# Queries of layers 1 to 3 as one pair in step: four of seven products by seven of their own

## The chip, the cores and the metric

The kernel runs on one core of one Trainium2 chip. The metric is the device time of one execution in microseconds. The kernel before takes 2476.75 us, the median of three runs (2476.53 to 2476.88).

## The reference

The program is a small graph network with four attention layers. `x` has 1024 rows of 512; `cond` has 16 sequences of 256 rows of 512; there are 8 heads of 64. Cut to what matters:

```python
def _attn(xf, cond, Wq, Wk, Wv, Wo):
    xb = xf.reshape(BS, n // BS, d)
    q = (xb @ Wq).reshape(BS, -1, H, DH)
    k = (cond @ Wk).reshape(BS, -1, H, DH)
    v = (cond @ Wv).reshape(BS, -1, H, DH)
    att = jnp.einsum('bnhd,bmhd->bhnm', q, k) * DH ** (-0.5)
    w = jax.nn.softmax(att, axis=-1)
    o = jnp.einsum('bhnm,bmhd->bnhd', w, v).reshape(BS, -1, H * DH)
    return (o @ Wo).reshape(n, d)

h = _gcn(batchnorm(relu(layernorm(x))), src, dst, gcn_in_w, gcn_in_b, n)
for i in range(L):                                   # L = 4
    h = h + _attn(_ln(h, ln2_w[i], ln2_b[i]), cond, Wq[i], Wk[i], Wv[i], Wo[i])
    u = _ln(h, ln3_w[i], ln3_b[i]) @ geglu_w[i] + geglu_b[i]
    val, gate = jnp.split(u, 2, axis=-1)
    h = h + (val * gelu(gate)) @ ffo_w[i] + ffo_b[i]
out = x + _gcn(h, src, dst, gcn_out_w, gcn_out_b, n) + x_in
```

All data is 32-bit floating point. The change concerns `q = _ln(h) @ Wq`, the factor `DH ** -0.5`, and what stands around them at the start of layers 1 to 3.

## The kernel before, in words

Seven products for eight. Each large product of the layers is cut into two by two blocks and made from seven products of blocks instead of eight, after Strassen and Winograd: sums of the left blocks, sums of the right blocks, seven products, and sums of the results on their way out of PSUM. A product over a block is a `multiply` (L297 to L305): two matmuls, one for each half of the contraction, for each 128 output rows. A 32-bit matmul appears in the profile as two records.

In step. Of the seven products, four (numbers 0, 5, 6, 4, in the list `INNER`) can be cut once more in the same way. `InStep` does this: `seven_of` runs seven inner products for two outer products at a time, each 128 x 256 wide, and `run` copies their sums back into PSUM banks, on top of which the three remaining outer products (1, 3, 2) add. The class `Pair` uses it for the gated unit (runs r of 1 to 3) and `KeyPair` for the keys of later attention steps. `inner_left` and `inner_right` (L963, L970) make the sums that this needs; they run on GpSimd (POOL). `Pair` keeps its intermediate results in the tile `wos`, which in the attention part holds the sums of `Wo` (`wo_sums`, L836).

One layer. There are 8 attention steps g, each for two sequences of `cond` and 128 rows of h. The start of layers 1 to 3 is written as: the keys and values of step 0 (`kv`), with the norms of the last blocks of h beside them; the transposes `turn_first` of the last four blocks, on whose way out of PSUM the norm's weight and bias columns (`cols`) are applied; the sums of the transposed inputs `lnT` into `lnS` (`sum_first`), for blocks 0 and 1 on POOL and for 2 and 3 on VectorE (DVE); POOL makes also the sums of `Wq` (`weight_sums`). Then the `queries`: two `QueryPair`s, one for each 128 rows of a block of q, with seven products of two matmuls of 512 columns each, the scale being applied in the evictions. Then `wo_sums` on POOL. Then the loop over the steps: `scores` (four banks of scores, the softmax's largest value and normalisation on DVE, exponentials on ScalarE, ACT), at g = 0 the keys and values of step 1, and then `mix`, which transposes the probabilities and multiplies by the values.

The order. Instructions run in order on each engine. The order on each engine is made by a scheduler when the program is built, from the program's order, a cost model and tile dependencies; `tc.issue_after`, `waiting_for` and `tc.keep_in_program_order` bind it. Tiles come from pools: `slots` (36 pieces of 128 x 1024), `work` (10 of 128 x 512, `t512`), `accs` (6), and 8 banks of PSUM. SyncE (SP) issues nearly all DMAs, in order.

For layer 0 the keys of step 1 already stand before the queries; it keeps its form of the queries.

Of the kernel before, what the change touches and what calls it, by code (L numbers as in the profile page):

```python
# [17 lines left out]
P = 128  # L18
# [5 lines left out]
def gnn_kernel(  # L24
# [76 lines left out]
    def slots_of(n, name):  # L101
        return [slot(f"{name}_{i}") for i in range(n)]
# [641 lines left out]
    def values(l, g, wv, begun=None, **also):  # L744
        v, s1 = begun or (slots_of(2, f"v_{l}_{g}"), None)
        v11, v21, v12, v22 = blocks_out(v)
        seven(f"v_{l}_{g}", of_v(wv, conds[l, g]), v11, v12, v21, v22, s1, **also)
        return v
# [218 lines left out]
        sums_of_a(t, *blk, s1, s2, s4)  # L967
        return order7(blk, s1, s2, s4)

    def inner_right(t, b11, b12, b21, b22, room):  # L970

        t1, t2, t3, t4 = (room[:, k, j * M:(j + 1) * M] for k in range(2) for j in range(2))
        for to, of, less in ((t1, b12, b11), (t3, b22, b12), (t2, b22, t1), (t4, b21, t2)):
            t.tensor_tensor(to, of, less, OP.subtract)  # L974
        return [b11, b21, b22, t4, t1, t2, t3]
# [4 lines left out]
        return {i: inner_left(nc.gpsimd, left[i], *rooms[3 * n:3 * n + 3])  # L980
                for n, i in enumerate(INNER[0] + INNER[1])}

    def inner_right_of(i, right, room):
        return inner_right(nc.gpsimd, *(right[i][:, k, n * M:(n + 1) * M]
                                        for k in range(2) for n in range(2)), room)

    class InStep:

# [66 lines left out]
    class Pair(InStep):  # L1055
# [38 lines left out]
        def upper(self, q, d, w7):  # L1094
            self.of_upper[q] = self.gated(q, d, w7, "g1")
# [54 lines left out]
    def cond_rights(l, g):  # L1150

        rooms = slots_of(4, f"kr_{l}_{g}")
        of = conds[l, g], conds[l, g + 1]
        return {i: inner_right(nc.gpsimd, *(x[i][:, k, :] for k in range(2) for x in of), room)
                for i, room in zip(INNER[0] + INNER[1], rooms)}

    def pairs_of(l, r, left, right, inner):
# [73 lines left out]
        product(2, d, False)  # L1231
        add(h12, d)

    class QueryPair:


        def __init__(self, l, c, left, right, qT):
            self.n, self.c, self.left, self.right = f"{l}_{c}", c, left, right
            (self.q11, self.q21), (self.q12, self.q22) = ([qt[d][:, c, :] for d in range(2)]
                                                          for qt in qT)  # L1240

        def product(self, i, to, start):
            multiply(to, self.left[i], self.right[i],
# [2 lines left out]
        def first(self):  # L1246
            self.a = bank(f"qa_{self.n}")
            self.product(0, self.a, True)
            self.s1 = acc_tile(f"qs1_{self.n}")
            nc.scalar.mul(self.s1, self.a, DH ** -0.5)  # L1250

        def second(self):
            self.product(1, self.a, False)
            nc.scalar.mul(self.q11, self.a, DH ** -0.5)

        def rest(self):
            def add(to, of, term):
                nc.vector.scalar_tensor_tensor(to, of, DH ** -0.5, term, OP.mult, OP.add)

            b, c, d = (bank(f"{x}_{self.n}") for x in ("qb", "qc", "qd"))  # L1260
            u2, u3 = (acc_tile(f"{x}_{self.n}") for x in ("qu2", "qu3"))
            self.product(5, b, True)
            add(u2, b, self.s1)
            self.product(6, c, True)
            add(u3, c, u2)
            self.product(4, d, True)
            add(self.q22, d, u3)
            self.product(3, c, False)
            add(self.q21, c, u2)
            self.product(2, d, False)  # L1270
            add(self.q12, d, u2)

    def queries(l, wq):
        qT = [slots_of(2, f"qT_{l}_{i}") for i in range(2)]
        right = [lnT[0][0], lnT[0][1], lnT[1][1], lnS[2], lnS[0], lnS[1], lnT[1][0]]
        pairs = [QueryPair(l, c, wq, right, qT) for c in range(2)]
        for q in pairs:
            q.first()
        for q in pairs:
            q.second()  # L1280
        for q in pairs:
            q.rest()
        return qT

    def sum_first(t, nb):

        c0 = nb % 4 * P
        of = [lnT[i][k][:, :, c0:c0 + P] for k in range(2) for i in range(2)]
        return sums_of_b(t, *of, *(x[:, :, c0:c0 + P] for x in lnS))
# [23 lines left out]
    def turn_first(l, blocks):  # L1313

        for nb in blocks:
# [3 lines left out]
            else:  # L1319
                pt = transposed(xn, f"hT_{nb}")  # L1320
                for k in range(2):
                    nc.scalar.copy(lnT[nb // 4][k][:, :, c0:c0 + P],
                                   four(pt)[:, 2 * k:2 * k + 2, :])

    lnT = [slots_of(2, f"ln2T_0_{i}") for i in range(2)]
    aggregate(parts_in, "in", into_h_and_norm)
    graph.close()
# [34 lines left out]
    for l in range(L):  # L1362

        wk, wv, wq, wo, ffb, spare = projections
        if l:
            lnS = slots_of(3, f"ln2S_{l}")
            kv_next = kv(l, 0, wk, wv, lambda _: ready_first(l, left_to_turn[2:]))
            with waiting_for(scaled.last, mybir.EngineType.Pool):
                sum_first(nc.gpsimd, 0)
                sum_first(nc.gpsimd, 1)  # L1370
                wq = weight_sums(wq, f"wqs_{l}")
                summed = weight_sums.last
            turn_first(l, left_to_turn)
            next_cond(l, 1)
            sum_first(nc.vector, 2)
            sum_first(nc.vector, 3)
        else:
            lnS = slots_of(3, f"ln2S_{l}")
            roots = []

            def root_beside(ins):
                with tc.issue_after(ins.ins):
                    roots.append(deviations(mv_first[1], "ln2_0_4"))

            kT, last_key = keys(0, 0, wk, begun["k0"], root_beside)
            with tc.issue_after(last_key.ins):
                scale_first(1, *roots)
            turn_first(0, [0, 1, 2, 3])
            with waiting_for(scale_first.last, mybir.EngineType.Pool):
                wq = weight_sums(wq, "wqs_0")  # L1390
            kv_next = kT, values(0, 0, wv, begun["v0"])
            turn_first(0, [4, 5, 6, 7])
            sum_first(nc.gpsimd, 0)
            summed = sum_first(nc.gpsimd, 1)
            kT_1, last_key = keys(0, 1, wk, begun["k1"])
            with tc.issue_after(last_key.ins):
                sum_first(nc.vector, 2)
                sum_first(nc.vector, 3)
        qT = queries(l, wq)
        with tc.issue_after(summed.ins):  # L1400
            wo7 = wo_sums(wo)

        ln3T, ln3S, right = [], [], []

# [67 lines left out]
        for g in range(NG - 1):  # L1472
# [26 lines left out]
            if l and g % 2:  # L1499
                with waiting_for(scores.last, mybir.EngineType.Pool):  # L1500
                    key_rights = cond_rights(l, g + 1)

                def kept_moments(ins):
                    if g > 1:
                        with tc.issue_after(ins.ins):
                            moments_into(mv_kept[:, 2 * (g - 3):2 * (g - 1)], [h[g - 3], h[g - 2]],
                                         f"ln3_{l}_{g - 3}")

                vs[g + 1] = values(l, g + 1, wv, beside=kept_moments)
            elif l and g:  # L1510
                turned = range(g) if g == NG - 2 else []
                if turned:
                    with waiting_for(scores.last, mybir.EngineType.Pool):
                        left = geglu_weights(l, 0, *raw)
                vs[g + 1] = values(l, g + 1, wv, late=lambda: [ln3_turn(nb) for nb in turned])
                next_cond(l, g + 2)
                next_cond(l, g + 3)
            else:
                if g or l:
                    kT, vs[g + 1] = kv(l, g + 1, wk, wv, between,  # L1520
                                       late=lambda: [ln3_turn(nb) for nb in ready])
                else:
                    kT, vs[1] = kT_1, values(0, 1, wv)
                kTs[g + 1] = whole(kT)
                save_conds()
                next_cond(l, g + 2)
                if l:
                    next_cond(l, g + 3)
                    spare.append(rows.tile([P, D], F32, tag="last", name=f"spare_{l}"))
                    wk_lefts = inner_lefts(wk, [x[:, i * P:(i + 1) * P] for x in spare  # L1530
                                                for i in range(4)])
# [48 lines left out]
        for r in range(R):  # L1580
# [7 lines left out]
            if r:  # L1588
                fT, fS, quads = pairs_of(l, r, left, right, (lefts, rights))
            else:  # L1590
                wff = []

                rooms = slots_of(4, f"gr_{l}")

                def beside(c):
                    with waiting_for(quads[c].last, mybir.EngineType.Pool):
                        if c < 2:
                            for i in INNER[c]:
                                rights[i] = inner_right_of(i, right, rooms.pop(0))
                    if c == 2:  # L1600
                        wff.extend(out_weights(nc.vector, l, 0, raw_out))

# [83 lines left out]
```

## Time and profile before

| | us |
|---|---|
| runs, median of three | 2476.75 |
| the profiled execution | 2477.14 |
| its span, from the first to the last instruction | 2475.4 |
| TensorE (PE) busy | 2454.0 |
| DVE busy | 1543.6 |
| POOL busy | 807.9 |
| ACT busy | 692.4 |

PE is the matmul stream, PEld the weight loads that run beside it. In a timeline a row has the start in us from the span's start, the length, the engine, the line in the kernel, the operation, output <- inputs, shapes, and the count of instructions merged into the row; in brackets stands how long the engine was idle before it and what ended that. The lengths of TensorE's records overlap from one to the next, since matmuls are pipelined: the distance from start to start is what one costs. In a table of stretches, each row has the stretch, its length, and the busy time and count of PE, PEld, DVE, ACT and POOL, then the granted clock of TensorE, the share of DMA and GB/s. In a table of groups stand the count, the busy time and the mean length of one in ns. In a row of waits stand the total in us, the number of times and the longest.

### The profile page before, as it was taken

The page shows a single profiled execution, that of the slowest core. Times are in us where ns is not written, and L with a number is a line of the kernel's source. Part 1 is how long each engine was busy: PE and PEld are TensorE (multiplying, and loading weights), DVE is VectorE, ACT ScalarE, POOL GpSimd, SP SyncE. Part 2 cuts the span into 40 slices and gives each one's busy share as a digit, 9 for nine tenths or more (in the row PEclk, how much of TensorE's full clock was granted, in tenths as well). Part 3 has the DMA queues.
Part 4 walks back from the last instruction along what each step waited for, and adds up shares of the span by engine and source line. Part 5 has one row for each costly group of instructions (what it writes and reads, how often), then busy time and mean ns, then how long its engine had stood idle before and what let it go on. Part 6 is the DMA issues. An engine that isn't in the chain of part 4 may idle for free. (4 is left out here: it accounts for less than half of the span.)

```text
span 2475.4 us, 33973 instructions
## 1 busy us (share of the span) xinstructions
PE 2454.0 (99%) x12968; PEld 1865.6 (75%) x12968; DVE 1543.6 (62%) x3199; ACT 692.4 (28%) x1564; POOL 807.9 (33%) x883
## 2 busy tenths in 40 slices
PE   7999999999999999999999999999999999999999
PEld 5678887677778887577787888477787888577775
DVE  9655656566675557666675556666684556666661
ACT  7322322122212334122212333222222333322221
POOL 0322223532432223533541224344522222544410
PEclk9999999999999999999999999999999999999999
DMA  5313223110212221111212222011121031111110
GB/s 178 133 39 107 98 76 105 52 35 17 98 35 77 86 68 61 35 50 35 88 45 73 73 77 69 23 46 51 35 98 69 27 111 52 52 51 52 52 68 35
DMA packets 70395, 162.97 MB, mean 66 GB/s; under 512 B 5880, under 2 KB 6208, under 8 KB 70224
## 3 DMA queue, kind: packets, MB, share of 16 engines
q1 hardware_dynamic: 68128, 155.28, 18.8%
q0 software_dynamic: 1376, 4.30, 0.5%
q8 instruction: 107, 1.75, 0.3%
q10 hardware_dynamic: 720, 1.11, 0.1%
q14 instruction: 64, 0.52, 0.1%
HBM read 137.60 MB, written 23.07 MB: 65 GB/s over the span
## 5 line engine op out<-in xcount | busy, mean ns | idle before, releaser
L220 POOL TENSOR_TENSOR ges<-wgate,wgate 128x1024 f32<-128x1024 f32 x16 | 37.7, 2354 | 438.5 <-DVE fs L1176 401.4
L780 ACT ACTIVATE pr<-sc,nmax 128x256 f32<-128x256 f32 x256 | 118.0, 473 | 157.8 <-DVE nmax L775 157.5
L302 PE MATMUL pa_v<-wv,ct 128*128 128x256 f32 x512 | 123.5, 383 | 0.0
L302 PE MATMUL fa<-wff,fT 128*128 128x256 f32 x512 | 121.6, 379 | 0.0
L302 PE MATMUL pc_v<-wv,ct 128*128 128x256 f32 x512 | 121.0, 379 | 0.0
L302 PE MATMUL pd_v<-wvs,ct 128*128 128x256 f32 x512 | 120.9, 379 | 0.0
L302 PEld LDWEIGHTS fa<-wff,fT 128*128 128x128 f32 x512 | 97.3, 190 | 21.8 <-issue 9.6
L302 PEld LDWEIGHTS pa_v<-wv,ct 128*128 128x128 f32 x512 | 95.6, 190 | 19.5 <-issue 6.2
L1010 ACT COPY gs<-ga 128x512 f32<-128x512 f32 x48 | 27.9, 582 | 287.7 <-PE ga L1003 287.7
L974 POOL TENSOR_TENSOR kr<-ct,ct 128x256 f32<-128x256 f32 x36 | 27.7, 769 | 245.5 <-DVE pr L785 245.5
L302 PEld LDWEIGHTS pd_v<-wvs,ct 128*128 128x128 f32 x512 | 97.3, 190 | 13.2
L302 PEld LDWEIGHTS pc_v<-wv,ct 128*128 128x128 f32 x512 | 96.7, 190 | 12.8
L302 PE MATMUL ga<-ln3T,wval 128*128 128x512 f32 x224 | 104.4, 594 | 0.0
L775 DVE TENSOR_REDUCE nmax<-sc 128x2 f32<-128x512 f32 x128 | 82.9, 679 | 31.5 <-PE sc L768 31.5
L1084 ACT ACTIVATE g<-g,gcols 128x512 f32<-128x512 f32 x96 | 69.3, 722 | 94.8 <-DVE g L1081 94.8
L785 DVE TENSOR_SCALAR pr<-pr,inv 128x256 f32<-128x256 f32 x256 | 81.2, 359 | 2.9
L1429 POOL TENSOR_TENSOR hall<-hall,ffb 128x512 f32<-128x512 f32 x32 | 40.0, 1273 | 117.5 <-DVE fs L1176 71.2
L1211 DVE TENSOR_TENSOR hall<-fd,hall 128x512 f32<-128x512 f32 x64 | 44.1, 689 | 54.2 <-PE fd L302 54.2
L302 PE MATMUL gc<-ln3S,wgate 128*128 128x512 f32 x160 | 75.2, 592 | 0.0
L1211 DVE TENSOR_TENSOR hall<-fc,hall 128x512 f32<-128x512 f32 x64 | 44.0, 687 | 41.6 <-PE fc L302 41.6
L302 PEld LDWEIGHTS ga<-ln3T,wval 128*128 128x128 f32 x224 | 41.3, 190 | 35.9 <-issue 34.4
L803 PEld LDWEIGHTS po<-pT,v 128*64 128x64 f32 x2048 | 62.3, 138 | 7.7 <-issue 7.7
(476 smaller groups left out, 6182.6 us busy)
## 6 DMA issues: line engine op xcount, KB each, us to landing
ct<-cond_dram SPq DMA_DIRECT2D x72, 512.0 KB, 5.4
wval<-in_L_gnn_geglu_w_dram SPq DMA_DIRECT2D x32, 512.0 KB, 3.8
wgate<-in_L_gnn_geglu_w_dram SPq DMA_DIRECT2D x32, 512.0 KB, 4.6
wff<-in_L_gnn_ffo_w_dram SPq DMA_DIRECT2D x32, 512.0 KB, 3.8
cond_dram<-ct SPq DMA_DIRECT2D x24, 512.0 KB, 3.1
cond<-in_L_gnn_cond_dram SPq DMA_DIRECT2D x32, 256.0 KB, 4.5
ct<-cond_dram SPq DMA_DIRECT2D x24, 256.0 KB, 5.7
wk<-in_L_gnn_Wk_dram SPq DMA_DIRECT2D x8, 512.0 KB, 4.2
```

The costliest lines, as they stand in the source:

```text
L220: t.tensor_tensor(s1, a21, a22, OP.add)
L302: each(nc.tensor.matmul(at, left[:, k, l0:l1], right[:, k, r0:r1], start=start and n == 0 and k == 0, stop=n == len(cols_of) - 1 and k == ...
L775: nc.vector.tensor_reduce(nmax, ps3, AX.X, OP.max, negate=True)
L780: nc.scalar.activation(pr3[:, a, :], ps3[:, a, :], AF.Exp, bias=nmax[:, a:a + 1], accum_out=tot[:, a:a + 1])
L785: scores.last = nc.vector.tensor_scalar(pr3[:, a, :], pr3[:, a, :], inv[:, a:a + 1], None, OP.mult)
L803: mix.last = nc.tensor.matmul(po[j * DH:(j + 1) * DH, n0:n0 + NPG], v[b][:, m, c * P + j * DH:c * P + (j + 1) * DH], pTs[j][:, at:at + NPG ...
L974: t.tensor_tensor(to, of, less, OP.subtract)
L1010: nc.scalar.copy(s1, a)
L1084: nc.scalar.activation(g, g, AF.Gelu, bias=gate)
L1211: nc.vector.tensor_tensor(to, halves_of(of), to, OP.add)
L1429: nc.gpsimd.tensor_tensor(h[nb], h[nb], ffb, OP.add)
```

## The change

The old `QueryPair` is renamed `QueryQuad` and stays in layer 0. A new `QueryPair(InStep)` makes the queries of layers 1 to 3: products 0, 5, 6 and 4 as two runs of seven inner products, then products 1, 3 and 2. Its inner sums are made on POOL: those of the weights (`wq_lefts`, 16 differences of 128 x 128, behind `weight_sums`) and those of the inputs (`rights`, 16 differences of 128 x 256, in eight pieces of `work`). It keeps its intermediate results in `wos`, so `wo_sums` moves behind it, in layers 1 to 3 to the first step behind the scores. The keys of step 1 are made in front of the queries in all layers, and step 0 of the loop makes the values alone. The scale `DH ** -0.5` leaves the evictions and is multiplied once into the first 32 columns of `cols`, the weights and biases of the norm ahead of the attention.

```diff
+    def quarters(room):
+        return [room[:, k, j * M:(j + 1) * M] for k in range(2) for j in range(2)]
-    def inner_right(t, b11, b12, b21, b22, room):
-        t1, t2, t3, t4 = (room[:, k, j * M:(j + 1) * M] for k in range(2) for j in range(2))
+    def inner_right(t, b11, b12, b21, b22, rooms):
+        t1, t2, t3, t4 = rooms
         for to, of, less in ((t1, b12, b11), (t3, b22, b12), (t2, b22, t1), (t4, b21, t2)):
...
+    def blocks_of_q(qT, c):
+        return [[qT[n][d][:, c, :] for n in range(2)] for d in range(2)]
-    class QueryPair:
+    class QueryQuad:
...
-            nc.scalar.mul(self.s1, self.a, DH ** -0.5)
+            nc.scalar.copy(self.s1, self.a)
...
-                nc.vector.scalar_tensor_tensor(to, of, DH ** -0.5, term, OP.mult, OP.add)
+                nc.vector.tensor_tensor(to, of, term, OP.add)
...
+    class QueryPair(InStep):
+        x = "q"
+        def __init__(self, l, left, right, inner, qT):
+            self.n, self.left, self.right, self.inner = f"{l}", left, right, inner
+            self.w = [wos[:, 2 * q:2 * q + 2, :] for q in range(2)]
+            self.to = [blocks_of_q(qT, c) for c in range(2)]
+        def step(self, i, k):
+            lefts, rights = self.inner
+            return lefts[i][k], rights[i][k]
+        def product(self, i, q, to):
+            multiply(to, self.left[i], self.right[i], [(q * P, (q + 1) * P, 0, 512)], False,
+                     tc.keep_in_program_order)
+        def first(self, q, a):
+            nc.scalar.copy(self.to[q][0][0], a)
+        def upper(self, q, d, w7):
+            nc.vector.tensor_tensor(self.to[q][1][1], d, w7, OP.add)
+        def lower(self, q, c, w7, a):
+            nc.vector.tensor_tensor(self.to[q][1][0], c, w7, OP.add)
+        def final(self, q, d):
+            nc.scalar.copy(self.to[q][0][1], d)
-    def queries(l, wq):
+    def queries(l, wq, lefts=None):
         qT = [slots_of(2, f"qT_{l}_{i}") for i in range(2)]
         right = [lnT[0][0], lnT[0][1], lnT[1][1], lnS[2], lnS[0], lnS[1], lnT[1][0]]
+        if lefts:
+            rooms = [t512(f"qr_{l}_{i}") for i in range(8)]
+            rights = {i: inner_right_of(i, right, [x[:, j * M:(j + 1) * M]
+                                                   for x in rooms[2 * n:2 * n + 2]
+                                                   for j in range(2)])
+                      for n, i in enumerate(INNER[0] + INNER[1])}
+            QueryPair(l, wq, right, (lefts, rights), qT).run()
+        else:
...
+    nc.vector.tensor_scalar(cols[:, :2 * L * KC], cols[:, :2 * L * KC], DH ** -0.5, None, OP.mult)
     lnT = [slots_of(2, f"ln2T_0_{i}") for i in range(2)]
...
                 wq = weight_sums(wq, f"wqs_{l}")
-                summed = weight_sums.last
+                rooms = [weight_sums.spare, *(t512(f"ql_{l}_{i}") for i in range(2))]
+                wq_lefts = inner_lefts(wq, [x[:, i * P:(i + 1) * P] for x in rooms
+                                            for i in range(4)])
             turn_first(l, left_to_turn)
             next_cond(l, 1)
             sum_first(nc.vector, 2)
             sum_first(nc.vector, 3)
+            kT_1, _ = keys(l, 1, wk)
+            qT = queries(l, wq, wq_lefts)
         else:
...
-        qT = queries(l, wq)
-        with tc.issue_after(summed.ins):
-            wo7 = wo_sums(wo)
+            qT = queries(l, wq)
+            with tc.issue_after(summed.ins):
+                wo7 = wo_sums(wo)
...
-                if g or l:
+                if g:
                     kT, vs[g + 1] = kv(l, g + 1, wk, wv, between,
                                        late=lambda: [ln3_turn(nb) for nb in ready])
                 else:
-                    kT, vs[1] = kT_1, values(0, 1, wv)
+                    kT, vs[1] = kT_1, values(l, 1, wv)
+                    if l:
+                        with waiting_for(scores.last, mybir.EngineType.Pool):
+                            wo7 = wo_sums(wo)
```

More of the change, by code (lines that the diff above doesn't have):

```diff
@@ L981, in inner_lefts, with inner_right_of @@
                 for n, i in enumerate(INNER[0] + INNER[1])}
-    def inner_right_of(i, right, room):
-        return inner_right(nc.gpsimd, *(right[i][:, k, n * M:(n + 1) * M]
-                                        for k in range(2) for n in range(2)), room)
+    def inner_right_of(i, right, rooms):
+        return inner_right(nc.gpsimd, *quarters(right[i]), rooms)
     class InStep:
@@ L1153, in cond_rights @@
         of = conds[l, g], conds[l, g + 1]
-        return {i: inner_right(nc.gpsimd, *(x[i][:, k, :] for k in range(2) for x in of), room)
+        return {i: inner_right(nc.gpsimd, *(x[i][:, k, :] for k in range(2) for x in of), quarters(room))
                 for i, room in zip(INNER[0] + INNER[1], rooms)}
@@ L1232, in ffn_out @@
         add(h12, d)
-    class QueryPair:
+    def blocks_of_q(qT, c):
+        return [[qT[n][d][:, c, :] for n in range(2)] for d in range(2)]
+    class QueryQuad:
         def __init__(self, l, c, left, right, qT):
             self.n, self.c, self.left, self.right = f"{l}_{c}", c, left, right
-            (self.q11, self.q21), (self.q12, self.q22) = ([qt[d][:, c, :] for d in range(2)]
-                                                          for qt in qT)
+            self.to = blocks_of_q(qT, c)
         def product(self, i, to, start):
@@ L1249, in first @@
             self.s1 = acc_tile(f"qs1_{self.n}")
-            nc.scalar.mul(self.s1, self.a, DH ** -0.5)
+            nc.scalar.copy(self.s1, self.a)
         def second(self):
             self.product(1, self.a, False)
-            nc.scalar.mul(self.q11, self.a, DH ** -0.5)
+            nc.scalar.copy(self.to[0][0], self.a)
         def rest(self):
             def add(to, of, term):
-                nc.vector.scalar_tensor_tensor(to, of, DH ** -0.5, term, OP.mult, OP.add)
+                nc.vector.tensor_tensor(to, of, term, OP.add)
             b, c, d = (bank(f"{x}_{self.n}") for x in ("qb", "qc", "qd"))
@@ L1266, in rest @@
             self.product(4, d, True)
-            add(self.q22, d, u3)
+            add(self.to[1][1], d, u3)
             self.product(3, c, False)
-            add(self.q21, c, u2)
+            add(self.to[1][0], c, u2)
             self.product(2, d, False)
-            add(self.q12, d, u2)
-    def queries(l, wq):
+            add(self.to[0][1], d, u2)
+    class QueryPair(InStep):
[18 more added lines that the diff above has]
+            nc.scalar.copy(self.to[q][0][1], d)
@@ L1274, in queries @@
+    def queries(l, wq, lefts=None):
         qT = [slots_of(2, f"qT_{l}_{i}") for i in range(2)]
         right = [lnT[0][0], lnT[0][1], lnT[1][1], lnS[2], lnS[0], lnS[1], lnT[1][0]]
[L1276 to L1282, printed above, removed]
+        if lefts:
[6 more added lines that the diff above has]
+        else:
+            quads = [QueryQuad(l, c, wq, right, qT) for c in range(2)]
+            for q in quads:
+                q.first()
+            for q in quads:
+                q.second()
+            for q in quads:
+                q.rest()
@@ L1598, in beside @@
                             for i in INNER[c]:
-                                rights[i] = inner_right_of(i, right, rooms.pop(0))
+                                rights[i] = inner_right_of(i, right, quarters(rooms.pop(0)))
                     if c == 2:
```

## The prediction

> **What bounds the kernel now.** I read the page's totals first, then who TensorE waited for, then the order of time around the queries of layer 1.
>
> ```profile
> span 2475.4 us, 33973 instructions
> PE 2454.0 (99%) x12968; PEld 1865.6 (75%) x12968; DVE 1543.6 (62%) x3199; ACT 692.4 (28%) x1564; POOL 807.9 (33%) x883
> PE hw_in L463 <- ACT h0T L455: 2.2, 1, 2.2
> ```
>
> TensorE is busy 99% of the span. Its waits of 2 us and more all lie ahead of layer 0; the row shown (us in total, times, longest), where it waits once for the normalised input, returns below. In the layers it waits for nobody. So the change is worth what it takes off TensorE, less every gap that it opens there. The other engines matter through such gaps alone. In order of time, layer 1:
>
> ```profile
> 722.54 1.91 PE L184 MATMUL tr_ln<-ident,xn_ln 128*128 128x128 f32 x16
> 724.29 7.03 PE L302 MATMUL qa<-ln2T,wq 128*128 128x512 f32 x16
> 731.16 1.88 PE L302 MATMUL qb<-ln2S,wqs 128*128 128x512 f32 x4
> 748.42 1.96 PE L768 MATMUL sc<-kT,qT 64*64 64x256 f32 x32
> 750.31 1.99 PE L302 MATMUL pa_k<-ct,wk 128*128 128x256 f32 x8
> 774.59 1.91 PE L184 MATMUL tr_pr<-ident,pr 128*128 128x128 f32 x16
> ...
> 1295.25 7.03 PE L302 MATMUL qa<-ln2T,wq 128*128 128x512 f32 x16
> 1319.38 0.88 PE L768 MATMUL sc<-kT,qT 64*64 64x256 f32 x12
> ...
> 1866.21 7.03 PE L302 MATMUL qa<-ln2T,wq 128*128 128x512 f32 x16
> 1890.34 1.96 PE L768 MATMUL sc<-kT,qT 64*64 64x256 f32 x32
> ```
>
> From the first query product to the scores pass 24.13 us in each of layers 1 to 3 (748.42 - 724.29, and so on), so what is found for layer 1 counts three times. A matmul of 32-bit data stands as two records. The queries have 28 matmuls of 512 columns, 56 records, and records of this width follow each other every 0.429 us ((731.16 - 724.29) / 16): 24.04 us, and 0.09 at the seam. There is no slack in it. Durations in the rows overlap; I count from start to start.
>
> **Removed and put in: TensorE.** Four of the seven products (16 matmuls of 512 columns) become, for each of two outer pairs, seven inner products of two matmuls of 256: 28 matmuls, 56 records. The other three products stay: 12 matmuls, 24 records of 512. The gated unit's pair already runs exactly this sequence, so its stretches are the price:
>
> ```profile
> 724.29:748.33 24.04, 24.04 (x58) 10.46 (x56) 11.69 (x24) 5.70 (x11) 2.45 (x2) 1.00 0.00 1
> 627.68:639.76 12.08, 12.08 (x57) 10.64 (x56) 8.08 (x12) 4.46 (x8) 11.85 (x15) 1.00 0.28 99
> 639.76:650.06 10.30, 10.30 (x25) 4.56 (x24) 6.19 (x11) 3.99 (x6) 0.30 (x1) 1.00 0.00 1
> ```
>
> The first row is the queries as they are, the second the two sets of seven, the third the last six products. 24.04 - 12.08 - 10.30 = 1.66, with the steps unrounded 1.65 us a layer, 4.95 in all. That is the whole gain that this change can have on TensorE. It is also, to a hundredth, the 0.2% (4.95 us) below which I call a difference none, since about that much is what a measurement of this kernel can tell from no change. So the forecast hangs on whether anything of it is lost.
>
> **Moved: the keys of the second step.** Their 28 matmuls, two ACT copies and five DVE adds go from behind the scores to in front of the queries; no DMA goes with them, and SP's order of issues is unchanged. Their cond tiles must be there 26 us earlier, at 724.29:
>
> ```profile
> 691.64 4.25 SPq L280 DMA_DIRECT2D ct<-cond_dram  x4
> DMA to landing us min/median/max: 2.1/5.1/18.6
> ```
>
> The last of the four is issued by 695.9 and even the slowest landing of the run, 18.6, makes 714.5. Free. Behind the scores now stand the values alone: the seam after the scores (0.10 us: 750.31 to the next product took 1.83 in place of 1.73) stays, with pa_v in it. The cover of the first softmax falls from 24 to 12 us. Step 1 of the same layer runs that way already:
>
> ```profile
> 778.44 1.96 PE L768 MATMUL sc<-kT,qT 64*64 64x256 f32 x32
> 784.70 0.62 DVE L785 TENSOR_SCALAR pr<-pr,inv 128x256 f32<-128x256 f32 x2
> 792.52 0.71 PE L184 MATMUL tr_pr<-ident,pr 128*128 128x128 f32 x5
> ```
>
> The probabilities are done 6.9 us behind the first score (784.70 + 0.62), the transposes begin 14.1 behind it, without a gap. ACT's last query copies and the table load before its exponentials come later than today; I put that at some 0.5 us, and 7 us are free. Cost 0.
>
> **Scale in the norm's columns.** The evictions lose a factor; DVE waits for TensorE ahead of each, so a shorter one gives nothing. One DVE instruction is added, in the set-up, between the last two row statistics:
>
> ```profile
> 734.80 0.69 DVE L1258 SCALAR_TENSOR_TENSOR qu<-qc,qu 128x512 f32<-128x512 f32 x1 [0.95 <-PE qc L302]
> ...
> 10.21 0.22 ACT L411 COPY cols<-pc 128x72 f32<-128x72 f32 x1 [3.40 <-PE pc L399]
> 11.35 0.30 DVE L152 BATCH_NORM_AGGREGATE x_mean<-st_x 128x2 f32<-128x6 f32 x2
> 11.68 0.17 DVE L134 TENSOR_SCALAR v_x<-x_mean 128x8 f32<-128x8 f32 x1
> ```
>
> Its input is there at 10.43, so DVE doesn't wait for it; but this chain ends in the 2.2 us for which TensorE waits, so its step counts: 0 if it fits between the two aggregates, 0.2 by one of the two steps from 11.35 to 11.68, rounded up. I take 0.1.
>
> **Added on POOL, and what it does to DVE.** Each layer gets 16 differences of 128x128 on the weights and 16 of 128x256 on the inputs, in the stretch where POOL now makes wo's sums. Those go behind the first scores, where nobody is near: they are due at the first pair of attention outputs, behind step 1's transposes (792.52 above), and behind them POOL has only the differences of step 2, which wait for the scores of step 1 anyway.
>
> ```profile
> 720.51 1.27 POOL L223 TENSOR_TENSOR wqs<-wq,wqs 128x512 f32<-128x512 f32 x1
> 724.21 2.61 POOL L841 TENSOR_TENSOR wos<-wo,wos 128x512 f32<-128x512 f32 x2
> ...
> 726.34 0.76 DVE L213 TENSOR_TENSOR ln2S<-ln2T,ln2T 128x256 f32<-128x256 f32 x1
> 727.34 0.41 DVE L214 TENSOR_TENSOR ln2T<-ln2T,ln2T 128x256 f32<-128x256 f32 x1
> 729.46 0.42 DVE L216 TENSOR_TENSOR ln2S<-ln2T,ln2S 128x256 f32<-128x256 f32 x1
> ```
>
> DVE makes eight sums here. The first takes 0.76 beside POOL, the others 0.41, because POOL stops at 726.8 (724.21 + 2.61). After the change POOL runs through this stretch. Where both engines work on SBUF operands today:
>
> ```profile
> 786.08 0.73 POOL L974 TENSOR_TENSOR kr<-ct 128x256 f32<-128x256 f32 x1
> 786.63 0.73 DVE L1448 TENSOR_TENSOR x_again<-x_again,bias_out 128x512 f32<-128x512 f32 x1
> 786.76 1.18 POOL L974 TENSOR_TENSOR kr<-ct,kr 128x256 f32<-128x256 f32 x1
> 787.39 1.10 DVE L1449 TENSOR_TENSOR x_again<-x_again,again 128x512 f32<-128x512 f32 x1
> 787.91 1.17 POOL L974 TENSOR_TENSOR kr<-ct,ct 128x256 f32<-128x256 f32 x1
> ...
> 683.09 0.90 POOL L220 TENSOR_TENSOR wvs<-wk 128x128 f32<-128x128 f32 x1
> 683.95 0.45 POOL L223 TENSOR_TENSOR wvs<-wks,wvs 128x128 f32<-128x128 f32 x1
> ...
> L1211 DVE TENSOR_TENSOR hall<-fd,hall 128x512 f32<-128x512 f32 x64 | 44.1, 689 | 54.2 <-PE fd L302 54.2
> ```
>
> They take turns: POOL's 0.73 becomes 1.18, each waiting for the other's instruction. One round of one POOL difference of 256 columns and one DVE sum of 512 takes 1.14 us (787.94 to 789.08). A DVE sum of 256 takes 0.28 less (0.41 against 0.69 on average): 0.86 a round; with a POOL difference of 128, another 0.28 less (0.45 against 0.73): 0.58.
>
> [...]
>
> So, in layer 1: POOL makes one small difference ahead of L223 (0.41, one start to the next), is done with L223 at 722.1, and has some 14 small ones left, ten of which are over when DVE begins at 726.34. DVE's eight sums then go with about four small differences (0.58 each) and four large ones (0.86); with the turn that stands between them (0.34), and 0.1 or so because the first eviction of the keys stands ahead of the last sum, they end at 726.34 + 0.34 + 2.32 + 3.44 + 0.1 = 732.5 to 732.8 in place of 729.9. Behind them DVE must do the moved keys' evictions. TensorE begins the keys at 724.29 and would start their sixth product, which adds into the bank of the third, 5 x 1.727 later at 732.92; DVE's second eviction (0.69), which reads that bank, stands behind the last sum and ends at 733.2 to 733.5. I take the later, a wait of 0.6 us. **What is late next:** nothing. The first seven products begin at 724.29 + 12.09 + 0.6 = 737.0 and their second wants the third difference of the second input at 737.8; from 732.8 POOL has two small and three large ones to that point, 732.8 + 0.9 + 3 x 0.73 = 735.9. The second seven wants its second product's last operand at 737.0 + 6.04 + 0.86 = 743.9, and POOL has it eight large ones later, at 741.7; the last key eviction is not due before the scores of step 1.
>
> Bounds of this wait: none if POOL's turns don't hold DVE's sums (they end at 730.7); 2.5 us if each of the eight meets a large difference with its full start-to-start step (a step of 0.68 from 786.08 to 786.76 and one of 0.33 make 1.02; 726.34 + 0.34 + 8 x 1.02 + 0.69 is 735.5). 0.6 is nearest to the rounds that the rows show: 1.8 us in three layers.
>
> **Sum.** -4.95 + 0.1 + 1.8 = -3.05. The profiled execution took 2477.14 us (span 2475.4 and 1.74 around it), 0.39 above the median of the runs, 2476.75. It gives 2474.1, against the median **2473.7 us**.
>
> **Rivals.**
> 1. DVE's sums aren't late, or the eviction is not what holds the bank: no gap, -4.95 + 0.1, 2471.9. For it: TensorE runs through all of today's pairs without a gap. Against: the rounds of 1.14 us. This lies on the edge of 0.2% (2471.8), so it falls to either side.
> 2. POOL's chain of 32 differences is late itself, and TensorE waits in front of the first seven. If the 16 small ones ran at 0.90 each, as the row at 683.09, the chain would come 16 x 0.45 = 7.2 us later, at 743.1, 5.3 past its due time and with the 0.6 5.9 us a layer: 2476.75 - 4.85 + 17.7 = 2489.6. It decides for slower from 3.3 us a layer, which is 0.74 us for each small one. Against: 0.90 is the price of a DVE instruction in front of each, and DVE has only eight such sums.
> 3. The pair does not run as tight as the gated unit's: between its preloads ACT has two copies to the queries that the other hasn't. One copy (0.6 us) in front of each of two last products makes 1.2 a layer, 3.6 more than the forecast: 2477.3, no change. Against:
>
> ```profile
> L1010 ACT COPY gs<-ga 128x512 f32<-128x512 f32 x48 | 27.9, 582 | 287.7 <-PE ga L1003 287.7
> ```
>
> Behind the last inner product stand two DVE adds and one such copy, 0.69 + 0.69 + 0.58 and 0.2 of latency, 2.2 us; the last two products come 8 records of 0.429 behind it, 3.4 us.
> 4. The saving isn't there, because a matmul of 256 columns is dearer than half of one of 512. Against: 12.08 us for 56 of them, at a granted clock of 1.00 (last columns of the stretches).
>
> **How the numbers follow.** Forecast 0.52, own range 2472.5 to 2475.5; first rival 0.30, half of it below 2471.8; second 0.08; third 0.08; fourth 0.02. Faster 0.16 (half of the first, and a little of the forecast), slower 0.09, within 0.2% 0.75. The range goes from the first rival, 2471.5, to short of the third's price, 2477.0.
>
> **What would show it.** Right: the queries take 22.4 us from the first qa to the scores; DVE's ln2S sums behind the transposes lengthen from 0.41 to between 0.7 and 1; the keys' sixth product starts late by 0.3 to 1 us, and no other gap is there. Wrong: sums that end near 730 (first rival), a gap in front of qb (second), gaps before the last four query products (third).

## The result, and the profile after

| | before | after |
|---|---|---|
| median, us | 2476.45 (12 runs, 2475.32 to 2476.88) | 2482.33 (12 runs, 2481.71 to 2485.07) |
| the profiled execution, us | 2477.14 | 2482.07 |

The change makes the kernel slower: ratio 1.0026, 95% interval 1.0017 to 1.0035. The forecast was 2473.7, no change; the time lies 8.6 us above it and 5.3 above the end of its range. The page of the kernel after, its totals, and the row of its list of waits that the list of before doesn't have:

```profile
span 2480.3 us, 34302 instructions
PE 2452.6 (99%) x13040; PEld 1882.0 (76%) x13040; DVE 1573.1 (63%) x3224; ACT 709.4 (29%) x1594; POOL 863.3 (35%) x979
...
PE pc_k L302 <- DVE u_k L728: 7.1, 3, 2.4
```

TensorE's busy time fell by 1.4 us, and TensorE waits 7.1 us more, in three equal pieces, one in each of layers 1 to 3: for DVE's second eviction of the moved keys. The same place in order of time, TensorE in layer 1:

```profile
722.72 1.89 PE L302 MATMUL pa_k<-ct,wk 128*128 128x256 f32 x8
724.45 1.89 PE L302 MATMUL pb_k<-ct,wks 128*128 128x256 f32 x8
...
729.63 1.89 PE L302 MATMUL pa_k<-ct,wk 128*128 128x256 f32 x8
733.89 1.99 PE L302 MATMUL pc_k<-ct,wk 128*128 128x256 f32 x8 [2.36 <-DVE u_k L728]
...
737.44 0.59 PE L1005 MATMUL qa<-ln2T,wq 128*128 128x256 f32 x2
...
758.11 1.88 PE L302 MATMUL qb<-ln2T,wqs 128*128 128x512 f32 x4
759.92 1.31 PE L768 MATMUL sc<-kT,qT 64*64 64x256 f32 x20
```

From the first query product to the scores now pass 22.48 us (759.92 - 737.44) where 24.13 passed, without a gap. So the saving of 1.65 a layer is there, to the hundredth. But the keys' sixth product, due at 731.36 (729.63 + 1.73), starts at 733.89. DVE and then POOL at that place, from their timelines:

```profile
724.77 4.31 DVE L213 TENSOR_TENSOR ln2S<-ln2T,ln2T 128x256 f32<-128x256 f32 x1
729.01 0.40 DVE L698 TENSOR_SCALAR ln2T<-tr_ln,cols 128x128 f32<-128x128 f32 x1
729.33 0.62 DVE L214 TENSOR_TENSOR ln2T<-ln2T,ln2T 128x256 f32<-128x256 f32 x1
729.87 0.67 DVE L215 TENSOR_TENSOR ln2S<-ln2T,ln2S 128x256 f32<-128x256 f32 x1
...
732.07 0.68 DVE L725 TENSOR_TENSOR u_k<-pb_k,s_k 128x512 f32<-128x512 f32 x1
732.67 0.56 DVE L216 TENSOR_TENSOR ln2S<-ln2T,ln2S 128x256 f32<-128x256 f32 x1
733.15 0.68 DVE L728 TENSOR_TENSOR u_k<-pc_k,u_k 128x512 f32<-128x512 f32 x1
```

```profile
724.62 0.48 POOL L220 TENSOR_TENSOR ql<-wqs 128x128 f32<-128x128 f32 x1
725.03 0.48 POOL L223 TENSOR_TENSOR ql<-wq,ql 128x128 f32<-128x128 f32 x1
...
727.37 0.76 POOL L977 TENSOR_TENSOR qr<-ln2T 128x256 f32<-128x256 f32 x1
728.05 1.62 POOL L977 TENSOR_TENSOR qr<-ln2T,qr 128x256 f32<-128x256 f32 x2
```

DVE's first sum takes 4.31 us where it took 0.76 (4.29 in layers 2 and 3). Through all that time POOL runs one difference right behind another, 0.41 from start to start for a small one, as if nobody else were there: there are no turns. None of these differences needs the result of the one just ahead of it. DVE gets in only at the pair of POOL's last row above, which takes 1.62 instead of 1.4: there the second difference needs the result of the first (`inner_right` makes t4 from t2). From there the two do alternate (0.62, 0.67). The sums end at 733.23, not at 732.5 to 732.8, and the first key eviction (L725), which stands ahead of the last of them, begins at 732.07, though its product was over at 726.34 (724.45 + 1.89).

A second loss stands behind the gap. The stretches from the start of the sixth product to the first query product, one for each layer (the third number from the end is the granted clock):

```profile
733.89:737.44 3.55, 3.55 (x16) 3.14 (x17) 1.38 (x2) 0.00 (x0) 3.55 (x6) 1.00 0.00 0
1305.85:1311.10 5.25, 5.25 (x17) 4.33 (x18) 1.38 (x2) 0.00 (x0) 5.25 (x8) 0.67 0.00 0
1879.58:1884.82 5.24, 5.24 (x17) 4.32 (x17) 1.38 (x2) 0.00 (x0) 5.24 (x8) 0.67 0.00 2
```

Two products take 3.45 and a restart 0.10. In layer 1 that is all. In layers 2 and 3 the same 16 records take 1.70 and 1.69 longer at a granted clock of 0.67; in layer 3 the first eight take 3.47 (1879.58 to 1883.05), 0.43 each in place of 0.22. So TensorE was busy in that stretch, but slower, which hides most of the saving in its busy time. The account from the median of before: -4.95 saved, 3 x 2.4 of gap with its restart, and 1.69 for each layer with the lower clock: 2476.45 - 4.95 + 7.2 = 2478.7, with two such layers 2482.1, with three 2483.8. The runs lie from 2481.7 to 2485.1.

### The profile page after: what moved, and what is told of

It reads as the page before. It is cut to its first block, busy times and chain, and to the rows that moved or that the text cites. A ratio compares the mean times of both kernels' runs of the same rounds, so it can differ in the third digit from the quotient of the medians.

```text
span 2480.3 us, 34302 instructions
## 1 busy us (share of the span) xinstructions
PE 2452.6 (99%) x13040; PEld 1882.0 (76%) x13040; DVE 1573.1 (63%) x3224; ACT 709.4 (29%) x1594; POOL 863.3 (35%) x979
```

## The experiments

What was open: whether POOL's unbroken stream is what holds DVE, or the sums' place, the moved keys or the scale; and whether the lower clock belongs to the gap. All times are medians beside runs of the kernel before on the same chip: 2476.38 (33 runs) for the first four experiments, 2476.56 (24) for the next four, 2476.03 (18) for the last three.

**DVE's sums behind the keys' evictions.** DVE's eight sums go behind the keys' third eviction; all else as after.

```diff
-            sum_first(nc.vector, 2)
-            sum_first(nc.vector, 3)
-            kT_1, _ = keys(l, 1, wk)
+            def sums_beside(ins):
+                with tc.issue_after(ins.ins):
+                    sum_first(nc.vector, 2)
+                    sum_first(nc.vector, 3)
+            kT_1, _ = keys(l, 1, wk, None, sums_beside)
```

> The changed kernel with DVE's eight sums of blocks 2 and 3 in layers 1 to 3 put behind the third eviction of the moved keys. Theory (the sums, held off by POOL, make the second eviction late, and the gap that this opens lowers TensorE's clock): no gap in front of the keys' sixth product, granted clock 1.00 there, and the whole saving of 4.95 us is left: 2471 to 2472.5, ratio to before 0.998. Rival A (POOL's chain of differences is itself too late; the eviction was only the first to show it): the gap moves to the second in-step product of the queries, 1 to 3 us a layer, 2475 to 2482. Rival B (the clock falls for another reason than the gap): products at 0.43 us each in place of 0.22 near the keys although there is no gap.

Measured: 2471.39 (2470.61 to 2472.20), ratio 0.9980 (0.9971 to 0.9989): faster than both kernels, by the whole saving of 4.95. DVE and TensorE, layer 1:

```profile
728.72 0.69 DVE L728 TENSOR_TENSOR u_k<-pc_k,u_k 128x512 f32<-128x512 f32 x1 [0.96 <-PE pc_k L302]
730.45 0.69 DVE L730 TENSOR_TENSOR kT<-pd_k,u_k 128x512 f32<-128x512 f32 x1 [1.04 <-PE pd_k L302]
731.06 1.24 DVE L213 TENSOR_TENSOR ln2S<-ln2T,ln2T 128x256 f32<-128x256 f32 x2
732.22 0.41 DVE L214 TENSOR_TENSOR ln2T<-ln2T,ln2T 128x256 f32<-128x256 f32 x1
```

```profile
730.25 1.89 PE L302 MATMUL pa_k<-ct,wk 128*128 128x256 f32 x8
731.98 1.89 PE L302 MATMUL pc_k<-ct,wk 128*128 128x256 f32 x8
```

The eviction is done at 729.41, 2.6 us ahead of the product that needs its bank, and no gap is left. An eviction has one operand in PSUM and runs in 0.69 beside POOL's stream; only the sums, with both operands in SBUF, were held (4.31 for the first in the kernel after).

**The keys' move alone**, in the kernel before:

```diff
             sum_first(nc.vector, 2)
             sum_first(nc.vector, 3)
+            kT_1, _ = keys(l, 1, wk)
...
-                if g or l:
+                if g:
...
-                    kT, vs[1] = kT_1, values(0, 1, wv)
+                    kT, vs[1] = kT_1, values(l, 1, wv)
```

> The kernel before with one thing changed: the keys of step 1 in front of the queries in layers 1 to 3. No difference is added on POOL. Theory: POOL stops early as before, DVE's sums take 0.41 us each, no gap; 2476 to 2477, ratio 1.000. Rival (the moved evictions are late by themselves, because they stand behind the transposes' evictions and the sums): a gap of some 2 us a layer in front of the keys' sixth product, 2482 or more.

Measured: 2476.62 (2476.02 to 2477.64), ratio 1.0001 (0.9992 to 1.0010). In front of the queries too the keys leave no gap, as long as POOL is done: here DVE's first sum takes 0.73, one other 0.67, the rest 0.41, and the second eviction begins at 729.55.

**The scale alone**, in the kernel before:

```diff
-            nc.scalar.mul(self.s1, self.a, DH ** -0.5)
+            nc.scalar.copy(self.s1, self.a)
...
-                nc.vector.scalar_tensor_tensor(to, of, DH ** -0.5, term, OP.mult, OP.add)
+                nc.vector.tensor_tensor(to, of, term, OP.add)
...
+    nc.vector.tensor_scalar(cols[:, :2 * L * KC], cols[:, :2 * L * KC], DH ** -0.5, None, OP.mult)
     lnT = [slots_of(2, f"ln2T_0_{i}") for i in range(2)]
```

> The kernel before with the scale in the norm's columns alone. Theory: 0 to +0.2 us by one more DVE instruction in the set-up, 2476.5 to 2477. Rival (the 1.4 us by which the set-up of the changed kernel's profile is shorter belong to this edit): 2475 or less.

Measured: 2476.51 (2475.23 to 2477.11), ratio 1.0000 (0.9991 to 1.0009). The 0.1 of the forecast can't be told from nothing.

**POOL's small differences as a chain.** In the kernel after, the four differences of one product stand behind one another in an order in which most need the result just before them; DVE's sums stay in front of the evictions.

```diff
+            for to, a, b, op in ((s1, a21, a22, OP.add), (s2, s1, a11, OP.subtract),
+                                 (s4, a12, s2, OP.subtract), (a21, a11, a21, OP.subtract)):
+                tc.keep_in_program_order(nc.gpsimd.tensor_tensor(to, a, b, op))
```

> The changed kernel with the 16 differences of the query weights on POOL in an order in which nearly each one needs the result of the one ahead of it. Theory (POOL keeps DVE out as long as its instructions follow without a break; a wait for its own last result lets DVE in): the first of DVE's sums takes 1 us or less in place of 4.3, the gap in front of the keys' sixth product falls from 2.4 to some 0.5 us, no loss of clock: 2472.5 to 2475. Rival (POOL has precedence while it has any work left, or the order of its queue decides): first sum still 4 us and more, gap 2.4 us or more, 2481 to 2486.

Measured: 2471.93 (2470.49 to 2472.78), ratio 0.9981 (0.9972 to 0.9990): 4.45 us faster, which can't be told from the whole saving. DVE, then POOL, then TensorE, layer 1:

```profile
726.53 0.44 DVE L213 TENSOR_TENSOR ln2S<-ln2T,ln2T 128x256 f32<-128x256 f32 x1
726.90 0.40 DVE L698 TENSOR_SCALAR ln2T<-tr_ln,cols 128x128 f32<-128x128 f32 x1
727.22 0.41 DVE L214 TENSOR_TENSOR ln2T<-ln2T,ln2T 128x256 f32<-128x256 f32 x1
727.55 0.67 DVE L215 TENSOR_TENSOR ln2S<-ln2T,ln2S 128x256 f32<-128x256 f32 x1
```

```profile
725.71 0.45 POOL L995 TENSOR_TENSOR ql<-wq 128x128 f32<-128x128 f32 x1
726.24 0.46 POOL L995 TENSOR_TENSOR ql<-ql,wq 128x128 f32<-128x128 f32 x1
726.77 0.52 POOL L995 TENSOR_TENSOR ql<-wq,ql 128x128 f32<-128x128 f32 x1
727.25 0.69 POOL L995 TENSOR_TENSOR wq<-wq 128x128 f32<-128x128 f32 x1
727.90 0.63 POOL L995 TENSOR_TENSOR ql<-wqs 128x128 f32<-128x128 f32 x1
```

```profile
731.40 1.89 PE L302 MATMUL pa_k<-ct,wk 128*128 128x256 f32 x8
733.13 1.89 PE L302 MATMUL pc_k<-ct,wk 128*128 128x256 f32 x8
```

The work is the same, and so are its two engines; POOL's steps of 0.53 in place of 0.41 show it waiting for its own results. DVE gets in at once (0.44 in place of 4.31), and now they do take turns, in rounds of 0.6 to 0.9, as the forecast had it. The sixth product starts 1.73 behind the fifth: no gap is left, where 0.5 us had been expected. So the gap comes from the order in which POOL's differences stand, and turns begin where POOL waits for its own result. They can begin elsewhere too: in the first experiment DVE's first sum, at 731.06, got in between two of POOL's differences that start 0.41 apart and need nothing of each other:

```profile
730.97 0.45 POOL L221 TENSOR_TENSOR wk<-wk 128x128 f32<-128x128 f32 x1
731.38 0.63 POOL L221 TENSOR_TENSOR wks<-wks 128x128 f32<-128x128 f32 x1
```

What else lets DVE in is not shown.

**The changed kernel again**, for a second profile.

> The changed kernel once more, for a second profile. Theory (the gap of 2.4 us ahead of the keys' sixth product, and behind it in some layers a lower granted clock that costs 1.5 to 1.75 us): gaps of 2.3 to 2.5 us in all three layers; the time is 2471.9 + 7.2 = 2479.1 plus 1.5 to 1.75 for each layer whose records show the lower clock, so 2480.8 with one, 2482.4 with two, 2484 with three. Rival (the lower clock belongs to layers 2 and 3 and not to the gap's chance position): again exactly layers 2 and 3, 2482.4, and no run far from it.

Measured: 2482.69 (2481.78 to 2484.36), ratio 1.0026 (1.0015 to 1.0037); the profiled execution 2483.39. The gaps are 2.34, 2.29 and 2.35. The stretches behind them:

```profile
733.63:738.87 5.24, 5.24 (x16) 4.33 (x17) 1.39 (x2) 0.00 (x0) 5.24 (x8) 0.67 0.00 0
1307.23:1312.47 5.24, 5.24 (x16) 4.28 (x17) 1.38 (x2) 0.00 (x0) 5.24 (x8) 0.67 0.00 0
1880.89:1886.14 5.25, 5.25 (x17) 4.32 (x17) 1.38 (x2) 0.00 (x0) 5.25 (x8) 0.67 0.00 0
```

This time layer 1 has the lower clock too, and each time 1.69 or 1.70 us are lost (5.24 - 3.55). So it isn't a matter of the layer: it came behind five of the six gaps of the two profiles and behind one it didn't, and where it came it cost 1.69 or 1.70.

**Made gaps.** To part the gap from what DVE and POOL do there, the first experiment's kernel, which has none, was given one: further ACT copies of the bank into which the keys' fifth product adds, in layers 1 to 3.

```diff
             nc.scalar.copy(s1, a)
+            for _ in range(held):
+                nc.scalar.copy(c11, halves_of(a))
         product(5, b, True)
```

With ten copies:

> The kernel with DVE's sums behind the keys' third eviction, which has no gap (2471.4), and with ten more ACT reads of the bank into which the keys' fifth product adds: 0.53 to 0.58 us each behind the copy that ends at 726.1, so the fifth product starts at 731.4 to 731.9 in place of 730.25, a made gap of 1.2 to 1.7 us in each of layers 1 to 3, with POOL and DVE as they were. Theory (the clock falls only behind a gap long enough): granted clock 1.00 behind it, 2471.4 + 3.6 to 5.1, so 2475.0 to 2476.5. Rival (every gap costs its length and some two thirds of it again): 2477.4 to 2479.9.

With twelve:

> The same with twelve more reads: the fifth product at 732.4 to 733.1, a made gap of 2.2 to 2.9 us in each of layers 1 to 3, as long as that of the changed kernel but with nothing else of it. Theory (the gap itself lowers the granted clock behind it): records of 0.43 in place of 0.22 us behind two or three of the gaps, 2471.4 + 6.6 to 8.7 + 3.0 to 5.2, so 2481.0 to 2485.3. Rival (the clock fell because of what POOL and DVE do there, not because of the gap): granted clock 1.00, 2478.0 to 2480.1.

Measured: 2473.93 (2472.84 to 2474.92), ratio 0.9990 (0.9981 to 0.9999), and 2473.40 (2472.69 to 2474.83), ratio 0.9988 (0.9979 to 0.9997), both below all that was expected, because the gaps weren't made. TensorE with ten copies, layer 1:

```profile
729.46 1.46 PE L302 MATMUL pc_k<-ct,wk 128*128 128x256 f32 x6
731.39 2.00 PE L302 MATMUL pa_k<-ct,wk 128*128 128x256 f32 x8 [0.47 <-ACT kT L724]
```

The scheduler that orders the engines had put most of the sixth product ahead of the fifth, which left 0.5 us of the gap. The two runs answer only that gaps of 0.4 to 0.5 us bring no lower clock (1.00 over the whole run in both). For the next three the order of these products was held:

```diff
-    def of_k(w, right):
+    def of_k(w, right, each=lambda ins: ins):
         return lambda i, to, start: multiply(
-            to, w[i], right[i], [(c * P, (c + 1) * P, 0, M) for c in range(2)], start)
+            to, w[i], right[i], [(c * P, (c + 1) * P, 0, M) for c in range(2)], start, each)
...
+        order = [tc.keep_in_program_order] if l and g == 1 else []
```

> As the two kernels with more ACT reads, but with the order of the keys' products on TensorE held, since there another product had filled most of the gap. Nine reads at 0.615 us: the fifth product 1.3 us late in layers 1 to 3. Theory (the clock falls behind a gap long enough, and 1.3 us is not): granted clock 1.00, 2471.4 + 3 x 1.4 = 2475.6. Rival (each gap costs its length and some two thirds of it again): 2478.2.

> Eleven reads: the fifth product 2.55 us late in each of three layers, as long as the gap of the changed kernel, while DVE's sums and POOL stand as in the kernel without a gap. Theory (the gap itself lowers the granted clock behind it): records of 0.43 in place of 0.22 us for up to 3.4 us behind two or three of the gaps, 2471.4 + 3 x 2.65 + 2 or 3 x 1.7 = 2482.7 to 2484.4. Rival (the clock fell because of what DVE and POOL do at that place in the changed kernel): granted clock 1.00, 2479.3.

> Fourteen reads: 4.4 us late. Theory (one stretch of half the clock behind each gap, whatever the length of the gap): 2471.4 + 3 x 4.5 + 3 x 1.7 = 2490.0, with 1.7 us lost behind each gap. Rival (the loss grows with the gap, as two thirds of it): 3.0 us lost behind each, 2493.9. Without any loss it would be 2484.9.

Measured: 2475.45 (2475.14 to 2476.76), ratio 0.9998 (0.9989 to 1.0007); 2483.38 (2482.02 to 2485.92), ratio 1.0028 (1.0017 to 1.0038); 2492.99 (2492.53 to 2494.48), ratio 1.0068 (1.0054 to 1.0082). The stretches from the fifth product's late start to the first query product, where three products and the restart take 5.28: the one of layer 1 with nine copies, all three with eleven, all three with fourteen:

```profile
731.54:736.82 5.28, 5.28 (x24) 4.66 (x25) 3.53 (x9) 0.59 (x1) 3.24 (x5) 1.00 0.00 0
```

```profile
734.44:741.41 6.97, 6.97 (x24) 5.86 (x25) 2.27 (x6) 0.59 (x1) 5.74 (x9) 0.76 0.00 0
1308.15:1315.08 6.93, 6.93 (x24) 5.87 (x25) 2.26 (x6) 0.59 (x1) 5.71 (x9) 0.76 0.00 0
1881.82:1888.64 6.82, 6.82 (x24) 5.76 (x25) 2.25 (x6) 0.59 (x1) 5.60 (x8) 0.77 0.00 0
```

```profile
735.17:742.14 6.97, 6.97 (x24) 5.85 (x25) 0.69 (x1) 0.59 (x1) 6.97 (x11) 0.76 0.00 0
1310.73:1318.75 8.02, 8.02 (x25) 6.63 (x25) 0.69 (x1) 0.59 (x1) 7.88 (x12) 0.65 0.00 0
1887.34:1895.48 8.14, 8.14 (x25) 6.69 (x25) 0.69 (x1) 0.59 (x1) 7.90 (x12) 0.64 0.00 0
```

Gaps of 1.2 us, three times, lose nothing behind them. Gaps of 2.4, made by ACT's reads alone, with DVE and POOL as in the kernel without a gap, lose 1.69, 1.65 and 1.54, as there: the gap is the cause, and the rival of 2479.3 falls. Gaps of 4.3 lose 1.69, 2.74 and 2.86, which neither theory had expected of all three: by the time, 2493.0, the rival in which the loss grows with the gap came nearer (2493.9), but the first of the three lost 1.69, as one of 2.4 did. Where between 1.2 and 2.4 it begins was not tried, but the set-ups of the 13 profiles (before, after and the 11 runs of this section) narrow it. TensorE waits there twice for about 2 us, once for ACT's h0T and once for DVE's v_deg. In the 3.5 us behind the wait the granted clock is 1.00 in all 15 cases of 1.69 to 2.16 us, and lower in five of the 11 cases of 2.17 to 2.34 (0.70 in the profile before).

**The keys back behind the scores**, in the kernel after: the covering work taken away.

```diff
-            kT_1, _ = keys(l, 1, wk)
             qT = queries(l, wq, wq_lefts)
...
-                if g:
+                if g or l:
```

> The changed kernel with the second step's keys put back behind the scores, so that the queries follow the transposes. Theory (the keys are the cover of POOL's differences): the first set of seven wants differences of ln2S that POOL had at 733.8 in the changed kernel, while TensorE gets there some 1.3 us behind the transposes, at 725.7: a gap of 7 to 10 us in the first set of seven, some 0 to 2 in the second, no gap in the keys: 2471.9 + 3 x 7 to 12, so 2493 to 2508. Rival (POOL would be in time without the keys, and their move only brought the gap of 2.4): 2472 to 2474.

Measured: 2507.75 (2507.55 to 2509.30), ratio 1.0126 (1.0111 to 1.0142). The row of its list of waits, and TensorE in layer 1:

```profile
PE qb L1005 <- POOL qr L977: 27.4, 6, 5.0
```

```profile
729.72 0.95 PE L1005 MATMUL qb<-qr,wqs 128*128 128x256 f32 x2 [5.04 <-POOL qr L977]
734.95 1.22 PE L1005 MATMUL qb<-qr,ql 128*128 128x256 f32 x2 [4.27 <-POOL qr L977]
```

Both waits stand in the first set of seven, 9.3 us in this layer, and the second set has none. The keys are the cover of POOL's differences, and without them the change costs 31 us. The waits make 27.4 of the 35.8 us above the chain's kernel (2471.93); of the other 8.4, the lower clock in the stretch behind the second wait takes 7.0, by the profile: 5.25 x (1 - 0.50), 5.25 x (1 - 0.66) and 5.24 x (1 - 0.50) in the three layers. The first of these stretches:

```profile
734.95:740.20 5.25, 5.25 (x12) 4.20 (x13) 1.97 (x3) 0.00 (x0) 5.25 (x8) 0.50 0.02 3
```

At a granted clock of 0.50 it loses 2.6 us.

## Why the prediction was wrong

*Bound and saving: right.* The bound was TensorE's stream, the saving 1.65 us a layer. The two kernels in which nothing else happens lie at 2471.39 and 2471.93, where the forecast's first rival, no gap, stood at 2471.9.

*Keys, cover of the softmax, scale, wo's sums: right.* Each at nothing that can be measured, and where the keys stand is worth 9 us of wait a layer, which the forecast had used without naming its price.

*The place of the wait: right.* The keys' sixth product, for DVE's second eviction behind the sums, and no other wait.

*Its size: wrong, and here the forecast failed.* "They take turns" gave 0.6 us a layer; the rows show 2.4, just inside the upper bound of 2.5 (whose terms, 735.5 - 732.92, make 2.6). The rounds of 1.14 had been read from a stretch in which the two engines did alternate, and carried over to one in which POOL has a row of differences that are all ready. There POOL kept going, and DVE's first sum lasted 4.31 us. The chain experiment shows it: the same work with POOL waiting for its own results gives the forecast's turns, and no gap. The rounds of one stretch don't say which of the two is next in another, and that was the question: beside this sum one difference of POOL's takes 0.48 to 0.76, and the sum was held for 3.9 (4.31 - 0.41).

*"What is late next: nothing": wrong.* Late next was the clock. A gap was priced at its length; each of 2.3 to 2.4 us cost 1.54 to 1.70 more in eight of nine cases. The row was to be had in the profile before. Behind TensorE's 2.2 us wait for the normalised input, which the prediction shows, stands this stretch of the table of stretches:

```profile
26.00:33.00 7.00, 6.26 (x16) 2.59 (x17) 6.34 (x27) 6.13 (x14) 0.00 (x0) 0.76 1.01 131
```

A granted clock of 0.76 behind a wait of the length that was in question; it was not read. It would have shown a risk and not a sure loss: the other wait of that set-up, 2.16 us for DVE's v_deg, has 1.00 behind it. The gaps measured here, those of the changed kernel and the made ones, decide as far as they go: 2.3 to 2.4 us were enough in eight of nine cases, and 1.2 in none of three. Why a loss is near 1.7 us, and why layer 1 had it in one profile and not in the other, no run shows.

*The range: wrong by its own rule.* The wait's upper bound was kept as 2.5, and three of those alone make 2477.14 - 4.95 + 0.1 + 7.5 = 2479.8 of the profiled execution, above the 2477.0 at which the range ended.

*The rivals.* No gap (2471.9) is what the kernel does once the sums or POOL's order are mended. POOL's chain being late doesn't happen behind the keys, and does without them. Preloads late and a dearer matmul of 256: neither; there is no gap among the queries, and 56 records of 256 and 24 of 512 took what the gated unit's did.

## What to carry to other kernels

Where DVE works with both operands in SBUF beside POOL, ask whether POOL's instructions there are ready all at once: here such a row, eight differences long, held a sum of 0.41 for 4.31 us. So put what TensorE waits for ahead of DVE's SBUF work, or give POOL an order in which it waits for itself. Both are edits of a few lines, and either turned this change from 1.0026 into 0.998. And price a gap in a TensorE stream that is otherwise full not by its length alone: here 1.2 us cost 1.35, 2.4 cost 4.0, and 4.3 cost 7.2, by the medians over 2471.39.

## What the runs showed of the hardware

- One DVE sum of 128 x 256 with both operands in SBUF lasted 4.31 us in place of 0.41 through eight differences that POOL ran back to back, and 4.29 in the two other layers of that profile; POOL itself was hardly slowed in that time (0.41 from start to start). Where POOL waited for its own result, DVE got in at once (0.44). DVE's evictions, with one operand in PSUM, took 0.69 beside the same stream.
- The loss of clock behind a gap was 1.69 or 1.70 us in five of six layers of the changed kernel and none in the sixth, 1.54 to 1.69 behind made gaps of 2.4, none behind 1.2; behind 4.3 us 1.69 once and 2.7 to 2.9 twice. In the set-ups, waits of up to 2.16 us had none behind them, and waits of 2.17 to 2.34 in five of 11 cases. What decides between these was not settled.
- Runs of the two kernels without gaps lie within 1.6 us (2470.6 to 2472.2) and 2.3 us (2470.5 to 2472.8), those of the changed kernel within 3.4 and, run again, within 2.6.
